# Twelve state groups of a selective scan: states into PSUM, C products from GpSimd to VectorE

## The chip, the core and the metric

The kernel runs on one core of a Trainium2 chip. The metric is the device time of the whole program in microseconds (us), the median of several runs. Engines are named as in the profile: PE is TensorE, PEld its weight loads, DVE is VectorE, ACT is ScalarE, POOL is GpSimd, SP is SyncE, which here starts nearly all DMAs.

## What is computed

Two layers of an image network on a tensor of 4 batches, 384 channels and 32 x 32 positions, all in float32. The first layer is a selective scan in four directions followed by a mixture of experts (4 experts, 2 per token); the second is self-attention (8 heads of 64) followed by a feed-forward part. The change lies in the scan. Cut to that part, the reference is:

```python
xs = cross_scan(x)                       # 4 directions, 384 channels, 1024 positions
x_dbl = einsum('bkdl,kcd->bkcl', xs, x_proj_weight)
dts, Bs, Cs = split(x_dbl, [12, 16, 16])
dt = softplus(einsum('bkrl,kdr->bkdl', dts, dt_projs_weight) + bias)
for l in range(1024):                    # 16 states n of each channel d
    h = h * exp(dt[l] * A) + (dt[l] * u[l]) * B[l]
    y[l] = sum_n(h * C[l])
```

Here A is one number per channel and state. After it come the sum of the directions, a normalisation, GELU and the residual.

## The kernel before

**Layout of the scan.** The 384 channels are 12 blocks of 32 channels; the 16 states are 4 *state groups* (NG) of 4 states. A block of 32 channels with 4 states fills the 128 partitions. A *unit* is a batch, a direction k (in the order 0, 1, 3, 2) and a half i of the 1024 positions (512 each), so a batch has 8 units; directions 2 and 3 run through the halves and the positions backwards. A unit has 3 *chunks* c of 128 channels (4 blocks, two pairs q), and each chunk goes through the 4 state groups g. A batch thus has 96 state groups (8 units x 3 chunks x 4), each with 4 blocks.

**One state group** (`chunk`, from L436): for each pair q, GpSimd multiplies dt times u with B for both blocks in one instruction (bx, L445, 128x1024). For each block j, ScalarE makes the decay exp(dt A) into a PSUM bank (da, L454); there are two such banks. VectorE runs the recurrence over 512 positions as a scan (L459), from zero or from the carried state of the half before. In the first half of a direction VectorE copies the last state to a small carry tile (L470 for q = 0, L465 for q = 1). Then the states are multiplied by C. For q = 0 the scan writes the states over bx in SBUF, and GpSimd multiplies both blocks by C in one instruction (L473, 128x1024). For q = 1 the scan writes the states over the decay in PSUM, and VectorE multiplies each block by C (L466, 128x512). GpSimd does not read PSUM anywhere in this kernel. At last four TensorE matmuls with a 0/1 matrix (L480) sum over the states into the chunk's accumulator acc (a PSUM bank), over the 4 groups. There are 6 buffers for bx, 7 for the loaded dt and dt times u (dtr), and 2 shared PSUM banks ("ps") for acc and the projections.

**Around it** (`scan_layer`): after a chunk's last group VectorE adds acc to y (L291 for direction 0, L295 for the others). The next unit's projection (`project`) is interleaved with the groups: a matmul for dt (L370), ScalarE steps of a softplus (L374 to L387), in the first batch TensorE sums (L383), in later batches GpSimd subtractions (L400, L401) and a VectorE addition (L407), then dt times x on VectorE (L408), and DMAs to and from DRAM (L410, L411, L429). After the last direction of a half, `finish` normalises and stores it (GpSimd addition L239).

**Order of the work.** A scheduler places each instruction in its engine's queue by a modelled timeline and priorities; each engine then runs its queue in that order. The rest of the network for batch b (the *tail*: routing, experts from L991 and L1013, attention from L1123, feed-forward) is placed after the scan of batch b and is interleaved with the scan of batch b + 1. In the first batch no tail runs beside the scan; the tail of the last batch runs alone at the end.

Of the kernel before, what the change touches and what calls it, by code (L numbers as in the profile page):

```python
# [58 lines left out]
NG = NS // NJ  # L59
# [58 lines left out]
class Body:  # L118
# [295 lines left out]
    def chunk(self, unit, first, c, fed, carry, nega, sel, acc, work, dap):  # L414

        nc = self.nc
        b, k, i = unit
        bcs, dd, _ = fed  # L420
        dtr = []
        for q in range(NJ // 2):

            pair = []
            at = c * P + q * 2 * DB
            for s in range(2):
                t = work.tile([P, 2, HF], F32, tag="dtr", name="dtr", bufs=7)
                for n in range(NJ):
                    nc.sync.dma_start(  # L429
                        out=t[n * DB : (n + 1) * DB],  # L430
                        in_=dd[s, at : at + 2 * DB, :].rearrange("(j d) l -> d j l", d=DB),
                    )
                pair.append(t)
            dtr.append(pair)

        def run(ap):  # L436
            return ap[:, ::-1] if k >= 2 else ap

        last = 0 if k >= 2 else HF - 1
        for g in range(NG):  # L440
            bc = bcs[g]
            out = []
            for q in range(NJ // 2):
                bx = work.tile([P, 2, HF], F32, tag="bx", name="bx", bufs=6)
                pool = nc.gpsimd.tensor_mul(  # L445
                    bx, dtr[q][1], bc[:, 0].unsqueeze(1).to_broadcast([P, 2, HF])
                ).ins
                cg = bc[:, 1]
                at = ((c * 2 + q) * NG + g) * 2
                for j in range(2):  # L450
                    block = c * NJ + 2 * q + j
                    col = (k * NB + block) * NG + g
                    da = dap.tile([P, HF], F32, tag="da", name="da")
                    nc.scalar.activation(  # L454
                        da, dtr[q][0][:, j, :], AF.Exp, scale=nega[:, col : col + 1]
                    )
                    hold = carry[:, at + j : at + j + 1]
                    h = bx[:, j, :] if q == 0 else da
                    nc.vector.tensor_tensor_scan(  # L459
                        run(h), run(da), run(bx[:, j, :]), 0.0 if first else hold,  # L460
                        ALU.mult, ALU.add,
                    )
                    if q == 1:
                        if first:
                            nc.vector.tensor_copy(hold, h[:, last : last + 1])  # L465
                        dve = nc.vector.tensor_mul(bx[:, j, :], h, cg).ins  # L466
                if q == 0:
                    if first:
                        for j in range(2):
                            nc.vector.tensor_copy(  # L470
                                carry[:, at + j : at + j + 1], bx[:, j, last : last + 1]
                            )
                    pool = nc.gpsimd.tensor_mul(  # L473
                        bx, bx, cg.unsqueeze(1).to_broadcast([P, 2, HF])
                    ).ins
                out.append(bx)
            for q in range(NJ // 2):
                for j in range(2):
                    lo = (2 * q + j) * DB
                    nc.tensor.matmul(  # L480
                        acc[lo : lo + DB, :], sel, out[q][:, j, :],
                        start=(g == 0), stop=(g == NG - 1),
                    )
            self.place_behind = {"pool": pool, "dve": dve}
            yield
# [1089 lines left out]
```

## Time and profile before

| what | value |
|---|---|
| median of 3 runs | 4209.68 us (4201.19 to 4214.02) |
| the profiled execution's own time | 4199.62 us |
| its span in the trace | 4197.9 us |
| mean granted TensorE clock | 0.877 |
| first GpSimd product of the scan starts | 44.13 us |
| seventh unit's last sum into y (VectorE) | 641.07 us |

The page of the profile has these slices (40 equal ones of 105 us; each digit is the busy share in tenths, 9 for 90% or more):

```profile
PE   6545454479987888789996887789996988999899
DVE  5999997878887877788887867788887862010101
ACT  5555555556665776776665776676665774421353
POOL 5999997898989877798989976888998961000100
PEclk8666666589998999799998998789998999999999
```

Three stages can be seen. Slices 2 to 7 or so are the first batch's scan, in which GpSimd and VectorE are busy and TensorE is half idle at a low granted clock. Then scan and tail run together, up to about slice 33. The last seven slices are the tail of the last batch, in which GpSimd and VectorE do nearly nothing. A busy row gives the engine's time, its share of the span and the number of instructions; a group's row gives line, engine, operation, output and inputs with shapes, the count, then busy time and mean ns of one, then the idle time of the engine just before these instructions and what ended most of it. TensorE has two records for each matmul.

### The profile page before, as it was taken

What the parts mean: (1) busy time and instruction counts of PE and PEld (TensorE: products, weight loads), DVE (VectorE), ACT (ScalarE), POOL (GpSimd) and SP (SyncE); (2) the same over time, 40 slices, a digit from 0 to 9 for tenths busy, and PEclk for the clock granted to TensorE, in tenths of its full rate; (3) what the DMA queues carried; (4) which work ended last, traced back from release to release, by engine and by line L of the source; (5) the groups of instructions that cost most, each with busy time, mean ns of one, the idle gap of its engine ahead of it and who ended that gap; (6) DMA issues with size and microseconds to landing.
All of it is one profiled execution on the core that took longest, in us unless ns stands there. A gap on an engine that the chain in (4) does not pass through costs nothing. (4 is left out here: it accounts for less than half of the span.)

```text
span 4197.9 us, 45862 instructions
## 1 busy us (share of the span) xinstructions
PE 3348.0 (80%) x13372; PEld 1574.9 (38%) x13372; DVE 2872.9 (68%) x4250; ACT 2463.8 (59%) x4485; POOL 3022.8 (72%) x1476
## 2 busy tenths in 40 slices
PE   6545454479987888789996887789996988999899
PEld 2101111145553223255553223245563224577423
DVE  5999997878887877788887867788887862010101
ACT  5555555556665776776665776676665774421353
POOL 5999997898989877798989976888998961000100
PEclk8666666589998999799998998789998999999999
DMA  5554464577986444577886434568887424356200
GB/s 139 126 136 124 111 176 111 154 226 217 254 249 179 103 131 120 170 213 228 233 252 192 112 105 137 153 195 241 224 249 220 109 64 170 122 179 208 88 6 31
DMA packets 378883, 677.67 MB, mean 161 GB/s; under 512 B 49920, under 2 KB 179328, under 8 KB 378624
## 3 DMA queue, kind: packets, MB, share of 16 engines
q1 hardware_dynamic: 368800, 647.42, 54.1%
q0 software_dynamic: 8192, 25.21, 1.9%
q8 instruction: 108, 1.77, 0.2%
q10 hardware_dynamic: 1632, 2.04, 0.2%
q14 instruction: 151, 1.24, 0.1%
HBM read 566.68 MB, written 107.79 MB: 161 GB/s over the span
## 5 line engine op out<-in xcount | busy, mean ns | idle before, releaser
L445 POOL TENSOR_TENSOR bx<-dtr,bcs 128x1024 f32<-128x1024 f32 x768 | 1795.4, 2365 | 189.1 <-PE acc L480 103.1
L454 ACT ACTIVATE da<-dtr,nega 128x512 f32<-128x512 f32 x1536 | 1044.5, 690 | 921.1 <-DVE bx L466 568.3
L473 POOL TENSOR_TENSOR bx<-bx,bcs 128x1024 f32<-128x1024 f32 x384 | 907.2, 2366 | 138.3 <-DVE carry L470 69.2
L480 PE MATMUL acc<-bx,sel 128*32 128x512 f32 x3072 | 495.4, 707 | 320.8 <-POOL bx L473 294.6
L991 PE MATMUL h_ps<-xc,w 128*128 128x256 f32 (+1 forms) x3168 | 652.3, 361 | 45.6 <-DMA w<-in_w 18.4
L1013 PE MATMUL y_ps<-w,hs 128*128 128x384 f32 x1824 | 630.2, 497 | 26.9 <-ACT hs L1004 18.7
L991 PEld LDWEIGHTS h_ps<-xc,w 128*128 128x128 f32 x3168 | 547.4, 196 | 202.4 <-issue 87.0
L459 DVE TENSOR_TENSOR_SCAN bx<-da,carry,bx 128x512 f32<-128x512 f32 x384 | 474.1, 1270 | 118.2 <-POOL bx L445 64.8
L459 DVE TENSOR_TENSOR_SCAN da<-da,carry,bx 128x512 f32<-128x512 f32 x384 | 475.9, 1273 | 77.6 <-ACT da L454 68.7
L459 DVE TENSOR_TENSOR_SCAN bx<-da,bx 128x512 f32<-128x512 f32 x384 | 451.9, 1210 | 95.1 <-POOL bx L445 54.7
L466 DVE TENSOR_TENSOR bx<-da,bcs 128x512 f32<-128x512 f32 x768 | 509.4, 680 | 3.9 <-DMA bcs<-both 0.4
L459 DVE TENSOR_TENSOR_SCAN da<-da,bx 128x512 f32<-128x512 f32 x384 | 455.2, 1218 | 68.8 <-ACT da L454 55.5
L1013 PEld LDWEIGHTS y_ps<-w,hs 128*128 128x128 f32 x1824 | 345.1, 193 | 305.3 <-issue 56.1
L1146 PE MATMUL s_ps<-w 64*128 64x512 f32 x1024 | 311.2, 663 | 76.6 <-ACT ex L1152 72.2
L1152 ACT ACTIVATE ex<-s_ps 128x512 f32<-128x512 f32 x512 | 300.7, 591 | 107.3 <-PE s_ps L1146 105.7
L1044 POOL DMA_INDIRECT got<-made,g_source x64 | 61.2, 957 | 401.1 <-PE h_ps L991 381.4
L999 ACT ACTIVATE hs<-h_ps,bb 128x256 f32<-128x256 f32 (+1 forms) x528 | 200.4, 441 | 240.5 <-PE h_ps L991 178.5
L1195 PE MATMUL o_acc<-ex,vt 128*64 128x512 f32 x1024 | 287.5, 639 | 23.2 <-ACT ex L1152 20.8
L480 PEld LDWEIGHTS acc<-bx,sel 128*32 128x32 f32 x3072 | 73.9, 116 | 611.2 <-POOL bx L473 404.8
L1146 PEld LDWEIGHTS s_ps<-w 64*128 64x128 f32 x1024 | 83.6, 190 | 287.3 <-ACT ex L1152 235.7
L370 PE MATMUL dt_ps<-xd,wdt 108*128 108x512 f32 x192 | 124.7, 736 | 59.5 <-ACT mag L409 30.5
L1017 DVE TENSOR_TENSOR y<-y_ps,bb 128x384 f32<-128x384 f32 x76 | 41.7, 549 | 170.0 <-PE y_ps L1013 170.0
(240 smaller groups left out, 3594.2 us busy)
## 6 DMA issues: line engine op xcount, KB each, us to landing
w<-in_w SPq DMA_DIRECT2D x352, 576.0 KB
dtr<-dd SPq DMA_DIRECT2D x1536, 128.0 KB
bcs<-both SPq DMA_DIRECT2D x512, 128.0 KB
dd<-one_e SPq DMA_DIRECT2D x96, 256.0 KB
dd<-mag SPq DMA_DIRECT2D x96, 256.0 KB
xt<-x SPq DMA_DIRECT2D x32, 384.0 KB
made<-y SPq DMA_DIRECT2D x32, 384.0 KB
xs<-rows SPq DMA_DIRECT2D x28, 385.0 KB
```

The lines of the kernel that those rows point to most:

```text
L445: pool = nc.gpsimd.tensor_mul(bx, dtr[q][1], bc[:, 0].unsqueeze(1).to_broadcast([P, 2, HF])).ins
L454: nc.scalar.activation(da, dtr[q][0][:, j, :], AF.Exp, scale=nega[:, col : col + 1])
L459: nc.vector.tensor_tensor_scan(run(h), run(da), run(bx[:, j, :]), 0.0 if first else hold, ALU.mult, ALU.add,)
L466: dve = nc.vector.tensor_mul(bx[:, j, :], h, cg).ins
L473: pool = nc.gpsimd.tensor_mul(bx, bx, cg.unsqueeze(1).to_broadcast([P, 2, HF])).ins
L480: nc.tensor.matmul(acc[lo : lo + DB, :], sel, out[q][:, j, :], start=(g == 0), stop=(g == NG - 1),)
L991: ins = nc.tensor.matmul(ps[:, r, :], w1[(f + r) // wf][:, c, (f + r) % wf * P : ((f + r) % wf + 1) * P], xc[:, c, :], start=(c == 0), sto ...
L999: done = nc.scalar.activation(hs[:, f + r, :], ps[:, r, :], AF.Gelu if last or alone else AF.Identity, bias=bb[:, f + r : f + r + 1],).ins
L1013: nc.tensor.matmul(out[:, :D], hs[:, f, t * P : (t + 1) * P], w2[f // wf][:, f % wf, :], start=(f == 0), stop=(f == FC - 1),)
L1146: ins = nc.tensor.matmul(ps, w[rows, j * P : (j + 1) * P], w[rows, halves(i)], start=True, stop=True).ins
L1152: done.append(nc.scalar.activation(ex[:, o, :], ps, AF.Exp, scale=HD**-0.5, accum_out=sums[:, t, 2 * j + o, i : i + 1],).ins)
L1195: ins = nc.tensor.matmul(out[cols, :], made[t][1][:, j, cols], ex[:, o, :], start=(j == 0), stop=(j == MB - 1),).ins
```

## The change

In the first batch (b = 0), in the last state group of a chunk (g = NG - 1), and where c + i < 2 (chunks 0 and 1 of half 0, chunk 0 of half 1, which is 3 of the 6 chunks of each direction, 12 in all), the pair q = 0 is treated as q = 1 is: the scan writes its states over the decay in PSUM, the carry is copied from there, and VectorE multiplies each block by C. The GpSimd product by C of that pair is gone. The rest of the program is the same; the scheduler orders it anew.

```diff
         for g in range(NG):
             bc = bcs[g]
             out = []
+            spare = b == 0 and g == NG - 1 and c + i < 2
             for q in range(NJ // 2):
+                in_psum = q == 1 or spare
...
                     hold = carry[:, at + j : at + j + 1]
-                    h = bx[:, j, :] if q == 0 else da
+                    h = da if in_psum else bx[:, j, :]
                     nc.vector.tensor_tensor_scan(
...
-                    if q == 1:
+                    if in_psum:
                         if first:
                             nc.vector.tensor_copy(hold, h[:, last : last + 1])
                         dve = nc.vector.tensor_mul(bx[:, j, :], h, cg).ins
-                if q == 0:
+                if not in_psum:
                     if first:
                         for j in range(2):
                             nc.vector.tensor_copy(
```

## The prediction

> **What bounds the kernel now.** I read the busy rows and the slices of the page first, then a table of 210 us stretches, then what VectorE and GpSimd wait for inside the first batch, then a few microseconds of VectorE in order of time. The page and its groups:
>
> ```profile
> PE 3348.0 (80%) x13372; PEld 1574.9 (38%) x13372; DVE 2872.9 (68%) x4250; ACT 2463.8 (59%) x4485; POOL 3022.8 (72%) x1476
> L445 POOL TENSOR_TENSOR bx<-dtr,bcs 128x1024 f32<-128x1024 f32 x768 | 1795.4, 2365 | 189.1 <-PE acc L480 103.1
> L473 POOL TENSOR_TENSOR bx<-bx,bcs 128x1024 f32<-128x1024 f32 x384 | 907.2, 2366 | 138.3 <-DVE carry L470 69.2
> L459 DVE TENSOR_TENSOR_SCAN bx<-da,carry,bx 128x512 f32<-128x512 f32 x384 | 474.1, 1270 | 118.2 <-POOL bx L445 64.8
> L459 DVE TENSOR_TENSOR_SCAN da<-da,carry,bx 128x512 f32<-128x512 f32 x384 | 475.9, 1273 | 77.6 <-ACT da L454 68.7
> L466 DVE TENSOR_TENSOR bx<-da,bcs 128x512 f32<-128x512 f32 x768 | 509.4, 680 | 3.9 <-DMA bcs<-both 0.4
> ```
>
> The whole-span shares mislead: TensorE leads only because it works alone after 3500 us. The stretches (busy time of each engine in each) show it:
>
> ```profile
> 210.00:420.00 210.00, 98.31 (x316) 22.99 (x312) 193.06 (x261) 110.86 (x173) 208.95 (x91) 0.64 0.50 130
> 420.00:630.00 210.00, 104.97 (x322) 26.63 (x322) 194.63 (x273) 111.55 (x174) 208.96 (x92) 0.66 0.54 144
> 1050.00:1260.00 210.00, 192.88 (x891) 121.83 (x891) 173.55 (x240) 139.17 (x223) 188.01 (x88) 0.97 0.88 252
> 3570.00:3780.00 210.00, 210.00 (x815) 137.20 (x814) 20.20 (x34) 68.63 (x111) 0.00 (x0) 1.00 0.48 152
> ```
>
> The columns are TensorE, weight loads, VectorE, ScalarE, GpSimd, then the granted TensorE clock, DMA share and GB/s. In the first batch, where nothing of the tail runs beside the scan, GpSimd is busy 208.95 of 210 us (99.5%) and VectorE 193 to 195 (92%). The first batch's scan runs from GpSimd's first product at 44 us to about 778 us. From 850 to 3400 us scan and tail overlap and no engine is full; after that TensorE is alone. The change works in the first batch, so that is the stage to read. How near is VectorE to being the bound there? What it waited for between 121 and 641 us (total us, times, longest):
>
> ```profile
> DVE bx L459 <- ACT da L454: 10.2, 51, 0.3
> DVE da L459 <- ACT da L454: 9.3, 8, 2.4
> DVE y L295 <- PE acc L480: 8.9, 9, 1.7
> DVE one_e L408 <- PE dt_ps L383: 4.5, 6, 1.2
> DVE y L291 <- PE acc L480: 3.3, 3, 1.8
> DVE bx L459 <- POOL bx L445: 2.8, 5, 1.8
> ```
>
> Busy there is 478.3 of 520 us. The 51 waits of 0.2 us belong to VectorE's own loop: there are two PSUM banks for the decays, so the next decay can be computed only when the product has let a bank go. In order of time, one state group:
>
> ```profile
> 308.95 1.27 DVE L466 TENSOR_TENSOR bx<-da,bcs 128x512 f32<-128x512 f32 x2
> 310.45 2.46 DVE L459 TENSOR_TENSOR_SCAN bx<-da,carry,bx 128x512 f32<-128x512 f32 x2 [0.24 <-ACT da L454]
> 312.83 2.44 DVE L459 TENSOR_TENSOR_SCAN da<-da,carry,bx 128x512 f32<-128x512 f32 x2
> 315.18 1.27 DVE L466 TENSOR_TENSOR bx<-da,bcs 128x512 f32<-128x512 f32 x2
> ```
>
> From product pair to product pair is 6.23 us: two scans into SBUF, two into PSUM, two products, and one gap of 0.24 us. GpSimd needs three products of 2.31 us each for a group (by starts: six took 13.93 us), 6.93 us. So the two engines stand 6.2 to 6.9, and VectorE also carries about 2 us per chunk of four groups (y, dt times x).
>
> **The change, part by part.** All 12 groups are the last group of a chunk; they lie in three of every six chunks of the first batch.
>
> *Taken from GpSimd:* 12 C products (L473) of 2.31 us, 27.7 us. All lie on the busy engine, but two of the twelve are in the scan's first unit (44 to about 140 us, by 48 scans), where GpSimd itself waited 7.5 us for VectorE.
>
> *Added to VectorE:* 24 products of 128x512. Two take 1.27 us in the lines above, and records overlap by some 0.08 us, as with the scans (2.44 us long, 2.35 from start to start), so 1.19 us a pair, 14.3 us. With them comes a second gap per group: the next block's decays wait for these products as they do for the others, 0.2 us by the 51 waits above, 2.4 us in all. Sum 16.7 us, or 1.4 us a group. The four blocks of a group then hold PSUM banks through scan and product; nothing else uses those two banks, so TensorE is not held by it.
>
> *Moved:* the scans' target, SBUF to PSUM. The rows say 1270 ns into bx and 1273 ns into da: 0.003 x 24 = 0.1 us. The Trainium skill speaks against the change here: Perfetto Trace Analysis, Optimizing Scalar/DVE Operations, gives a VectorE operation about 60 ns of access overhead on SBUF and about 125 ns on PSUM. By that rule 24 scans would cost 1.6 us more. The row is for the same instruction with only the target changed, so I take 0.1 us. The same section warns that offloading between VectorE and GpSimd might not help, as they share an SBUF read port. If each added product held GpSimd up for its length, 14.3 us of the 27.7 would be lost. SBUF — State Buffer, Who interferes with whom, narrows that to VectorE instructions with two SBUF inputs; the product reads h in PSUM and only C in SBUF. GpSimd's products took 2332 to 2427 ns in the first 660 us, beside 173 such VectorE products, which leaves no room for stalls of 0.6 us. I take nothing.
>
> *Waits:* the carry copies stay as many, from PSUM at 149 ns, from SBUF at 153 (medians of the first 660 us): nothing. The matmuls of the last group no longer wait for a GpSimd product. VectorE's y waits for the chunk's accumulation, which ends with just that product (12.2 us in 12 waits above): these waits should go in the changed chunks, and shrink in the others, since GpSimd comes ahead. The 4.5 us on dt_ps are of the same kind: that matmul stands in TensorE's queue behind accumulations that wait for GpSimd. DMAs stay as many. In the order of instructions, GpSimd makes six bx products in a row at the start of many chunks and then three C products; all six bx buffers are then out, so what is late next is VectorE's scans.
>
> **The sum, by stretch.** From 121 to 641 us (the first unit's last chunk and the units 2 to 7, with 8 changed groups) GpSimd would need 517.9 - 8 x 2.31 = 499 us. VectorE needs 478.3 busy, plus its own gaps (75 groups, as L473 runs 75 times there, x 0.2 = 15), plus 8 x 1.4 = 11: 504.5 us. So VectorE becomes the bound, and at best 520 - 504.5 = 15.5 us are gained. The queues are in fixed order, only three groups are buffered, and changed chunks (VectorE 4 x 6.23 + 2 + 1.4 = 28, GpSimd 11 x 2.31 = 25.4 us) lie among others (27 against 27.7), so I leave some 5.5 us of waits, about half of the 12.2 on y: gain 10 us. First unit: VectorE is already what GpSimd waits for; two changed groups here cost up to 2.8 us, partly covered by VectorE's own 5.7 us of waits for bx: loss 1 us. Last unit (682 to 778 us): GpSimd is full, as it also makes the next batch's softplus subtractions; two C products less, 4.6 us, VectorE has 13 of 118 us idle: gain 3 us. Between them, from 641 to 682 us, normalisation and loading of the next batch keep both waiting; that is a chain of its own and only moves earlier. Together 12 us, off the profiled execution's 4199.6 us (span 4197.9): 4187.6. The median of the runs shown is 4209.7, 10 us above that execution; the same gain gives 4198 us.
>
> What lies after is moved earlier whole if the order stays. It does not quite: TensorE's stream has the accumulations up to 75 places later among the tail's matmuls while the third batch is scanned, and the fourth batch's first normalisation 30 places later. I take nothing for that, and put it into the range.
>
> **The rivals.**
> 1. *The whole relief counts* (chance 0.22). If most of VectorE's gaps are only GpSimd's shadow, GpSimd stays the bound: 10 groups (8, and 2 in the last unit) x 2.31 = 23, less 1 in the first unit, 22 us, 4188 us. For it: 99.5% busy, no waits. Against: the gaps of 0.2 us wait for ScalarE, not GpSimd.
> 2. *VectorE was the bound in all but name* (0.15). Then gain and added work cancel: within 4 us, 4206 to 4212 us. For it: 92% plus 3% of own gaps. Against: 12.2 us of y waits.
> 3. *The new order costs more later* (0.19). One mechanism: in the third batch TensorE's queue holds accumulations behind up to 75 more of the tail's matmuls. The trace has two records to a matmul (3072 for 1536 accumulations), and the experts' first matmuls (L991) take 652.3 us for 3168 / 2, 0.41 us each; that is up to 31 us once, during which all six bx buffers stay taken, so GpSimd stops and then VectorE. Between 900 and 3400 us GpSimd already waits 85.7 us in 23 waits for such matmuls, the longest 16.9. A slowdown begins when more than 12 us is added; with 31, 4229 us. Against: tail matmuls that come earlier leave the queue emptier later.
> 4. *The change does not do what it says*: excluded by the order of instructions, which has 12 products less on GpSimd and 24 more on VectorE.
>
> **How the numbers follow.** The likeliest case, VectorE becoming the bound, has 0.44, with a gain of 6 to 17 us (4193 to 4204). A measurement of this kernel can tell about 0.3%, 12.6 us, from no change. Of the likeliest case 0.22 lies beyond that, with rival 1 it makes 0.44 faster; its other 0.22, rival 2 and the mild end of rival 3 (0.01) make 0.38 the same; the rest of rival 3 is 0.18 slower. Range: 4178 (rival 1 and a favourable order) to 4224 (most of rival 3).
>
> **What would show it.** In the changed profile L473 should have 372 instructions and L466 792, at unchanged 2366 and 680 ns. From 210 to 630 us VectorE should rise to 96 to 98% and GpSimd fall to about 96%; y waits should shrink below 6 us between 121 and 641 us; the seventh unit's last y, 641.07 us now, should come about 9 us earlier. Wrong would be: GpSimd still at 99% (rival 1), that time unmoved (rival 2), or an early gain that is lost after 900 us in GpSimd's waits for accumulations (rival 3).

## The result, and the profile after

| | before | after |
|---|---|---|
| median | 4205.4 us (5 runs) | 4314.73 us (5 runs) |
| ratio, 95% interval | | 1.0264 [1.025, 1.0279] |
| the profiled execution's own time (span) | 4199.62 us (4197.9) | 4320.2 us (4318.4) |

The changed kernel is 2.6% slower, about 110 us, where 12 us faster had been forecast. The median before differs from the 4209.7 us above because two more runs came in. The busy row and four groups of the page after (lines above 444 are shifted by 2 in the code):

```profile
PE 3383.0 (78%) x13372; PEld 1594.9 (37%) x13372; DVE 2909.5 (67%) x4274; ACT 2461.4 (57%) x4483; POOL 2994.1 (69%) x1464
L447 POOL TENSOR_TENSOR bx<-dtr,bcs 128x1024 f32<-128x1024 f32 x768 | 1791.3, 2361 | 229.2 <-PE acc L482 144.8
L475 POOL TENSOR_TENSOR bx<-bx,bcs 128x1024 f32<-128x1024 f32 x372 | 875.7, 2360 | 230.8 <-DVE carry L472 133.9
L461 DVE TENSOR_TENSOR_SCAN da<-da,carry,bx 128x512 f32<-128x512 f32 x396 | 491.7, 1274 | 90.6 <-ACT da L456 67.5
L468 DVE TENSOR_TENSOR bx<-da,bcs 128x512 f32<-128x512 f32 x792 | 525.7, 680 | 3.8
```

The work is as predicted: 12 C products less on GpSimd, 24 more on VectorE, and none of these instructions takes over 1 ns longer (2360, 1274, 680 ns; 2366, 1273, 680 before). What grew is the idle time in front of GpSimd's instructions, behind the second bar: 189.1 to 229.2 us before bx, 138.3 to 230.8 before the C products. In stretches of 210 us (columns as in the prediction):

```profile
210.00:420.00 210.00, 102.56 (x300) 24.33 (x292) 187.08 (x244) 101.60 (x159) 188.05 (x82) 0.68 0.46 120
420.00:630.00 210.00, 108.97 (x303) 26.49 (x304) 191.43 (x264) 109.77 (x171) 191.41 (x83) 0.72 0.50 129
```

In the first batch both engines are less busy than before: GpSimd 188 to 191 us for 209, and VectorE, which has more to do, 187 to 191 for 193 to 195. Neither is full, so neither is the bound. What VectorE and GpSimd waited for between 121 and 641 us (total us, times, longest) shows that they wait for each other; "carry" is the small copy right behind VectorE's scans, so a wait for it is a wait for the scans:

```profile
DVE bx L461 <- POOL bx L447: 13.4, 13, 2.2
DVE y L295 <- PE acc L482: 6.9, 8, 1.9
DVE da L461 <- POOL bx L447: 6.2, 4, 2.2
```

```profile
POOL bx L475 <- DVE carry L472: 22.3, 9, 3.9
POOL bx L475 <- DVE bx L461: 18.6, 8, 3.8
POOL bx L447 <- DMA dtr<-dd: 9.3, 4, 4.4
```

GpSimd waits 40.9 us for VectorE, in 17 waits, and VectorE 19.6 us for GpSimd's bx, also in 17. The third row, 9.3 us for the load of dt, is not the cause: it stands in run 5 below too (9.4 us), which loses nothing. Before, VectorE had waited 3.5 us for GpSimd's bx in this stretch, and GpSimd once for VectorE:

```profile
POOL bx L473 <- DVE carry L470: 1.1, 1, 1.1
```

One such place in the timeline after, GpSimd first:

```profile
256.14 4.66 POOL L447 TENSOR_TENSOR bx<-dtr,bcs 128x1024 f32<-128x1024 f32 x2
262.24 9.28 POOL L447 TENSOR_TENSOR bx<-dtr,bcs 128x1024 f32<-128x1024 f32 x4 [1.44 <-PE acc L482]
271.48 2.36 POOL L475 TENSOR_TENSOR bx<-bx,bcs 128x1024 f32<-128x1024 f32 x1
274.29 2.36 POOL L475 TENSOR_TENSOR bx<-bx,bcs 128x1024 f32<-128x1024 f32 x1 [0.46 <-DVE carry L472]
280.58 2.34 POOL L475 TENSOR_TENSOR bx<-bx,bcs 128x1024 f32<-128x1024 f32 x1 [3.93 <-DVE carry L472]
282.88 18.52 POOL L447 TENSOR_TENSOR bx<-dtr,bcs 128x1024 f32<-128x1024 f32 x8
```

```profile
282.42 0.68 DVE L468 TENSOR_TENSOR bx<-da,bcs 128x512 f32<-128x512 f32 x1
285.27 2.35 DVE L461 TENSOR_TENSOR_SCAN da<-da,bx 128x512 f32<-128x512 f32 x2 [2.17 <-POOL bx L447]
```

GpSimd has made the bx products of three groups in a row (all six buffers) and then makes their three C products. The third has to wait for VectorE's scans of its group (3.93 us). Only after it does GpSimd go on to the next group's bx, so VectorE, done with its products, waits 2.17 us in its turn. In the order of instructions GpSimd's queue had 3 runs of five or more bx in the first batch before, and has 23 after.

When VectorE starts the last sum into y of a unit tells where the loss arises. The two profiled executions differ by 120.5 us in span; 112.3 of them are there when the scan of the last batch ends (us):

| last sum of | before | after | later by |
|---|---|---|---|
| first batch, unit 2 | 222.8 | 235.1 | 12.3 |
| first batch, unit 7 | 641.1 | 677.5 | 36.4 |
| first batch, unit 8 | 759.3 | 810.6 | 51.3 |
| second batch, unit 8 | 1657.8 | 1734.8 | 77.0 |
| third batch, unit 8 | 2565.0 | 2660.4 | 95.3 |
| fourth batch, unit 8 | 3432.0 | 3544.3 | 112.3 |

More than half arises in the batches that the change doesn't touch. There, from 900 to 3510 us, GpSimd waits more than the kernel before did from 900 to 3400 us (85.7, 54.2 and 47.3 us for the same three; run 10 shows these rows):

```profile
POOL bx L447 <- PE acc L482: 119.8, 31, 20.1
POOL bx L475 <- DVE carry L472: 92.2, 38, 7.6
POOL bx L475 <- DVE bx L461: 64.4, 32, 5.4
```

### The profile page after: what moved, and what is told of

Same layout as the page of the kernel before. It is cut to its first block, busy times and chain, and to the rows that moved or that the text cites. A ratio compares the mean times of both kernels' runs of the same rounds, so it can differ in the third digit from the quotient of the medians.

```text
span 4318.4 us, 45877 instructions
## 1 busy us (share of the span) xinstructions
PE 3383.0 (78%) x13372; PEld 1594.9 (37%) x13372; DVE 2909.5 (67%) x4274; ACT 2461.4 (57%) x4483; POOL 2994.1 (69%) x1464
## 5 line engine op out<-in xcount | busy, mean ns | idle before, releaser
L447 POOL TENSOR_TENSOR bx<-dtr,bcs 128x1024 f32<-128x1024 f32 x768 | 1791.3, 2361 | 229.2 <-PE acc L482 144.8
L475 POOL TENSOR_TENSOR bx<-bx,bcs 128x1024 f32<-128x1024 f32 x372 | 875.7, 2360 | 230.8 <-DVE carry L472 133.9
L482 PE MATMUL acc<-bx,sel 128*32 128x512 f32 x3072 | 517.4, 706 | 307.6 <-POOL bx L475 243.0
L1015 PE MATMUL y_ps<-w,hs 128*128 128x384 f32 x1824 | 642.4, 505 | 48.4 <-ACT hs L1006 38.7
L461 DVE TENSOR_TENSOR_SCAN bx<-da,carry,bx 128x512 f32<-128x512 f32 x372 | 458.8, 1270 | 150.2 <-POOL bx L447 85.3
L461 DVE TENSOR_TENSOR_SCAN da<-da,carry,bx 128x512 f32<-128x512 f32 x396 | 491.7, 1274 | 90.6 <-ACT da L456 67.5
L468 DVE TENSOR_TENSOR bx<-da,bcs 128x512 f32<-128x512 f32 x792 | 525.7, 680 | 3.8
L461 DVE TENSOR_TENSOR_SCAN bx<-da,bx 128x512 f32<-128x512 f32 x372 | 439.7, 1210 | 114.6 <-POOL bx L447 72.2
L461 DVE TENSOR_TENSOR_SCAN da<-da,bx 128x512 f32<-128x512 f32 x396 | 471.8, 1219 | 57.3 <-ACT da L456 41.2
L1197 PE MATMUL o_acc<-ex,vt 128*64 128x512 f32 x1024 | 288.1, 638 | 28.1 <-ACT ex L1154 18.5
```

Of the source, the lines that this page charges most:

```text
L447: pool = nc.gpsimd.tensor_mul(bx, dtr[q][1], bc[:, 0].unsqueeze(1).to_broadcast([P, 2, HF])).ins
L461: nc.vector.tensor_tensor_scan(run(h), run(da), run(bx[:, j, :]), 0.0 if first else hold, ALU.mult, ALU.add,)
L475: pool = nc.gpsimd.tensor_mul(bx, bx, cg.unsqueeze(1).to_broadcast([P, 2, HF])).ins
L482: nc.tensor.matmul(acc[lo : lo + DB, :], sel, out[q][:, j, :], start=(g == 0), stop=(g == NG - 1),)
L1015: nc.tensor.matmul(out[:, :D], hs[:, f, t * P : (t + 1) * P], w2[f // wf][:, f % wf, :], start=(f == 0), stop=(f == FC - 1),)
L1197: ins = nc.tensor.matmul(out[cols, :], made[t][1][:, j, cols], ex[:, o, :], start=(j == 0), stop=(j == MB - 1),).ins
```

## The experiments

Two theories stood against each other: **O**, the scheduler's new order of the queues costs, the moved work nothing; **V**, VectorE's load costs. A third, **D**: a late first batch drags the others behind it. The change alters both the instructions and, through the scheduler, the order of all queues. To part them, the order was taken from the schedule of one kernel and imposed on the instructions of the other. The edit, the same in all kernels whose order is called pinned:

```diff
+def pinned(tc, nc, order):
+    traced = list(nc.cur_bb.bb.instructions)
+    how = mybir.DependencyInfo(mybir.DependencyClass.NoSync, mybir.DependencyReason.DATA)
+    for engine, text in order.items():
+        mine = [i for i in traced if str(i.engine).split(".")[-1] == engine]
+        at, before = 0, None
+        for step in array.array("h", zlib.decompress(base64.b85decode(text))):
+            at += step
+            if before is not None:
+                tc.add_manual_dep(mine[at], before.name, how, reason="order")
+            before = mine[at]
...
+        pinned(tc, nc, ORDER_OF)
         over = nc.values_load(flag[0:1, 0:1], min_val=0, max_val=1)
```

These edges fix only the order within a queue; no wait for another engine is added or taken. ORDER_OF holds one list of places per engine. The kernel before, pinned to its own order and otherwise unchanged, has no run of its own, but run 10 is just that up to 850 us: its first batch ends 1.6 us later (760.9 against 759.3), so the pinning itself costs next to nothing.

**1. The new instructions in the old order.**

> The changed kernel's instructions, every engine's queue pinned to the order of the kernel before; the 24 new products stand right behind their scans, the 12 GpSimd products are missing. If the new order is what costs (theory O), the loss goes and the predicted gain shows: 4190 to 4205 us, the seventh unit's last y at 630 to 636 us. If VectorE's added load itself costs (theory V), about 4300 us, that y near 677 us as in the changed kernel.

Measured: 4209.83 us against 4205.86 for the kernel before, ratio 1.0006 [0.9995, 1.0016]. The loss is gone, so V falls as the cause of the 110 us. The predicted gain is not there either. The stretch from 121 to 641 us, in the kernel before and here:

```profile
121.00:641.00 520.00, 254.97 (x796) 62.29 (x796) 478.34 (x636) 274.92 (x428) 517.91 (x225) 0.65 0.52 135
```

```profile
121.00:641.00 520.00, 256.35 (x784) 64.35 (x788) 484.50 (x648) 272.49 (x424) 494.15 (x215) 0.66 0.50 132
```

GpSimd fell from 517.9 to 494.2 us of 520 and VectorE rose to 484.5, yet the seventh unit's last y came 5.9 us later (647.0, where 630 to 636 had been expected).

**2. The old instructions in the new order.**

> The instructions of the kernel before, every queue pinned to the order of the changed kernel; each of the 12 C products stands on GpSimd behind the next group's first bx. Theory O: 4315 to 4350 us (the loss of the changed kernel, and 12 products more on GpSimd). Theory V: about 4205 us.

Measured: 4324.13 us, ratio 1.0279 [1.0263, 1.0295]. The instructions of the kernel before, without any of the change, are as slow as the changed kernel when they stand in its order.

**3 and 4. The order by parts.** The same, with the order changed over at the last scan of the first batch.

> The changed kernel in its own order until the last scan of the first batch, then pinned to the order of the kernel before. If each stretch's order costs for itself (theory O), only the first batch's loss of 36 to 45 us stays: 4240 to 4255 us. If a late first batch drags the later ones behind it (theory D), 4300 us or more.

Measured: 4256.29 us, ratio 1.0113 [1.0097, 1.0129].

> The changed kernel pinned to the order of the kernel before until the last scan of the first batch, then in its own order. Theory O: the 65 to 75 us that the later batches lost stay, less the gain of the first batch: 4255 to 4280 us. Theory D: about 4200 us.

Measured: 4274.77 us, ratio 1.0165 [1.0149, 1.0181]. The new instructions with the old order stood at 1.0006; the new order adds 1.07% in the first batch and 1.59% after it. With the 0.06% of the instructions that makes 2.72%, and the changed kernel has 2.64%: within the intervals the parts add up. A first batch that ends 48 us late hardly drags the others: in run 3 the delay was 47.9 us at its end and 55.6 at the end of the last. D falls. A lower TensorE clock does not explain the first batch's part: run 3's mean granted clock was 0.880 to 0.883, no lower than the 0.875 to 0.881 of the kernel before beside it. Run 4's was a little lower, 0.874 to 0.879 (0.873 to 0.874 in the changed kernel, where TensorE is busy 35 us longer for as many records); whether that is a cause or a result of the waits, no run tells.

**5. One rule in the first batch.** The scheduler is free again, with an edge for GpSimd's bx alone (last_c, set in a line not shown, is the group's C product, or nothing where the group has none):

```diff
+                with self.behind_c(b == 0):
-                pool = nc.gpsimd.tensor_mul(
-                    bx, dtr[q][1], bc[:, 0].unsqueeze(1).to_broadcast([P, 2, HF])
-                ).ins
+                    pool = nc.gpsimd.tensor_mul(
+                        bx, dtr[q][1], bc[:, 0].unsqueeze(1).to_broadcast([P, 2, HF])
+                    ).ins
...
+            self.c_products = [*self.c_products[-1:], last_c]
...
+    def behind_c(self, on):
+        if not on or len(self.c_products) < 2 or self.c_products[0] is None:
+            return nullcontext()
+        return self.tc.issue_after(self.c_products[0])
```

> The changed kernel with one rule for the first batch: the bx products of a state group are queued on GpSimd behind the C product of the group two before it; the scheduler does the rest. Every later batch then stands in exactly the order of the kernel before. If GpSimd's runs of six bx and three C products are the cause in the first batch (theory R), its 36 us go: 4195 to 4215 us, no difference from before that can be told. If VectorE's load in the first batch costs (theory V), 4235 us or more.

Measured: 4196.5 us against 4192.84, ratio 1.0007 [0.9995, 1.0019]. All 110 us are gone with a rule on one queue of one batch. It does this in two ways. In the first batch GpSimd's queue has 5 runs of five or more bx instead of 23. And in the later batches, which the rule doesn't touch, the scheduler now comes to the order of the kernel before: from 742 us on TensorE, VectorE, ScalarE and GpSimd have their instructions in the same order in both traces. The stretch from 121 to 641 us:

```profile
121.00:641.00 520.00, 263.58 (x798) 67.55 (x796) 493.18 (x659) 275.47 (x430) 500.01 (x217) 0.68 0.53 137
```

Here VectorE is at 493.2 us (95%), GpSimd at 500. Up to the seventh unit 4.7 us are gained (y at 636.4), the transition to the second batch comes earlier by as much, and in the eighth unit the gain is lost (761.2 against 759.3).

**6. The bunching alone.** The kernel before, pinned to its own order, with GpSimd's queue in the units 2 to 7 rewritten from b C b b b C b b C b b C per chunk (b for bx) to b b b b b b C C C.

> The instructions and the order of the kernel before, with one change: in the units 2 to 7 of the first batch GpSimd's queue is regrouped to six bx and then three C products, 24 times. Theory R: the first batch loses 30 to 45 us, 4235 to 4255 us. If GpSimd's order is harmless and other queues' order costs, below 4215 us.

Measured: 4260.18 us, ratio 1.0161 [1.0135, 1.0187], 59.8 us lost by the seventh unit. That is above the 30 to 45 us expected. Bunching is enough to cost what the first batch lost; that it costs more here than the 36 us in the changed kernel may come from the other queues, which were ordered along with GpSimd's there and stand as before here. GpSimd's C products now wait for VectorE's scans, and VectorE's y, which stands at its old place, waits for acc, to which the late C products lead (143 to 690 us):

```profile
POOL bx L473 <- DVE carry L470: 23.1, 5, 6.9
POOL bx L473 <- DVE bx L459: 22.5, 5, 6.9
DVE y L295 <- PE acc L480: 45.8, 9, 7.2
DVE bx L459 <- POOL bx L445: 13.5, 13, 2.1
```

**7. One group of twelve.** `spare = b == 0 and g == NG - 1 and c + i == 0 and k == 0`, the scheduler free.

> Only one of the twelve groups is changed (direction 0, chunk 0, half 0), the scheduler is free. By the work alone 1.4 us more on VectorE: 4207 us. Theory O (what the scheduler makes of a shifted timeline decides): the first two units, where GpSimd's queue is bunched, lose 5 to 10 us, the later batches change by tens of us either way, so anything from 4210 to 4310 us and not 4207.

Measured: 4255.52 us, ratio 1.0147 [1.0124, 1.017], some 62 us. In the profiled execution, the slowest of the four (4270.2 us), the first batch lost 6 us (unit 2: 6.7, unit 7: 6.2), since the bunching dies out after two units; the batches after it lost 62 more by the last y. One changed group, by the prediction's sum about 1.4 us of work, gave the later batches another order, and that cost 1.3%. Part of the cost may lie on ScalarE: in this order its queue has 142 loads of a function table (ACT_TABLE_LOAD in the profile), 15 more than before, at 1.28 us each. The changed kernel has 125 loads, two less than before, so its own loss has another source.

**8. The rule in all batches**, in the kernel before and in the changed one.

> The kernel before with the rule in all batches: bx of a group behind the C product of the group two before it, the scheduler does the rest. If runs of bx also cost in the later batches: faster, 4150 to 4195 us. If there the room to run ahead covers waits for TensorE: slower, 4215 to 4260 us.

Measured: 4205.47 us against 4192.84, ratio 1.0035 [1.002, 1.0049]. Neither of the two ranges: the later batches neither gain from the rule nor lose much.

> The changed kernel with the rule for bx in all batches. The later batches of the kernel before under this rule lost 8 us net; if the rule fixes the order there too, the new instructions change nothing: 1.003 to 1.005 of the kernel before. If the order of the later batches is again another one, any value from 0.995 to 1.02.

Measured: 4223.56 us against 4203.77, ratio 1.0043 [1.0028, 1.0058]. Next to 1.0035 the new instructions again change nothing that can be told.

**9. Relief and load apart**, both pinned to the old order, to see why the gain of run 1 is missing:

```diff
-                    pool = nc.gpsimd.tensor_mul(
-                        bx, bx, cg.unsqueeze(1).to_broadcast([P, 2, HF])
-                    ).ins
+                    if not (b == 0 and g == NG - 1 and c + i < 2):
+                        pool = nc.gpsimd.tensor_mul(
+                            bx, bx, cg.unsqueeze(1).to_broadcast([P, 2, HF])
+                        ).ins
```

> The kernel before in its own order, with the twelve C products left out on GpSimd and put nowhere (the states of these blocks go unmultiplied into the sum). The relief alone. If GpSimd was the bound of the first batch: 18 to 23 us gained there, about 0.995 of the kernel before. If VectorE was as near to being the bound as its waits for ScalarE say (15 us of its 41 us idle): 8 us gained or less, 0.998 to 1.000.

Measured: 4195.87 us against 4203.77, ratio 0.9984 [0.9975, 0.9993], 6.7 us by the ratio.

```diff
                         dve = nc.vector.tensor_mul(bx[:, j, :], h, cg).ins
+                        if b == 0 and g == NG - 1 and c + i < 2:
+                            dve = nc.vector.tensor_mul(bx[:, j, :], h, cg).ins
```

> The kernel before in its own order, with 24 VectorE products more: in the same twelve groups each product of the pair q = 1 is made twice (the same value into the same place), and GpSimd keeps all its work. The load alone. If VectorE had room: within 4 us, 1.000 to 1.001. If it had none: 14 to 17 us in the first batch, 1.003 to 1.004.

Measured: 4215.37 us, ratio 1.0025 [1.0015, 1.0035], 10.5 us, between the two ranges. Over the whole time relief and load together make 1.0009, and run 1 found 1.0006. In the first batch alone they don't add: at the y of its eighth unit the relief gave 8.6 us and the load took 4.6, which would be a gain of 4, and run 1, with both, was 4.0 us late. What run 1 has besides is the second wait for a decay in each changed group; from 121 to 641 us VectorE waits 22.3 us for decays (70 waits) where it had waited 19.5 us (59 waits). That is 3 of the 8 us; the rest stays open. So does the rest of the load's time, which arose later (10.5 us late at the end of the second batch, 18.5 at the end of the third).

**10. TensorE's order in the later batches.** The kernel before in its own order; on TensorE alone, from the second batch's first expert matmul on, the accumulations of a chunk's first three groups stand up to two tail matmuls later (by the trace some 740 accumulations moved, most of them by two).

> The kernel before in its own order, but from the second batch's first tail matmuls on, on TensorE alone, the accumulations of a chunk's first three groups stand up to two of the tail's matmuls later. By the third rival of the prediction (accumulations behind tail matmuls keep the bx buffers taken) GpSimd's waits for acc grow from 86 us, and the run is 10 to 40 us slower. If GpSimd is not sensitive to them: within 5 us.

Measured: 4267.07 us against 4203.77, ratio 1.0139 [1.0124, 1.0153], far above the 10 to 40 us. GpSimd's waits from 900 to 3400 us, before and here:

```profile
POOL bx L445 <- PE acc L480: 85.7, 23, 16.9
POOL bx L473 <- DVE carry L470: 54.2, 21, 8.6
POOL bx L473 <- DVE bx L459: 47.3, 22, 6.7
```

```profile
POOL bx L445 <- PE acc L480: 146.0, 35, 15.9
POOL bx L473 <- DVE carry L470: 52.2, 20, 8.6
POOL bx L473 <- DVE bx L459: 33.7, 17, 4.2
```

The row for acc alone grows by 60 us, about what the run lost (58). The mechanism of the third rival is real and steep. In the changed kernel that row grew by 34 us and the two rows for VectorE by 55, so its later loss is not that mechanism alone. Which queue's order makes how much of it stays open.

## Why the prediction was wrong

**Bound now.** Half right. GpSimd was at 99.5% and almost without waits, but taking 27.7 us from it is worth 6.7 us (run 9). VectorE, at 92% and with gaps of its own, was nearly as close to the bound; the prediction's sum had seen this (504.5 of 520 us) and still left 10 us of gain.

**The added and the removed work.** The counts and durations were right, the 0.003 us for the scans' target too (1274 ns into PSUM, 1270 into SBUF). The 1.6 us that the prediction estimated from the Trainium skill (Perfetto Trace Analysis, Optimizing Scalar/DVE Operations) are not seen; the scan reads its decay from PSUM in both forms, so its output alone may not call for them. GpSimd's products did not get longer, so the warning of the shared port did not apply. The terms of the sum were mis-sized: together they are worth +2.5 us (1.0006, interval from -2 to +7 us), not -12. The step that failed there was "I leave some 5.5 us of waits, about half of the 12.2 on y: gain 10 us". In the old order the seventh unit's y came 5.9 us later (run 1); in a fitting order 4.7 us were gained by the seventh unit (run 5). "Last unit: gain 3 us" failed as well: in run 5 the last unit lost the 4.7 us again and 1.9 us more; GpSimd waited 6.5 us for VectorE there (677 to 800 us), where the kernel before had waited 1.2 us (682 to 800 us). For the instructions alone, rival 2 was right.

**The order.** The step that decided was "What lies after is moved earlier whole if the order stays. It does not quite: ... I take nothing for that". After the first batch the new order is worth 1.59% (about 67 us). In the first batch it is worth 1.07% (about 45 us), and there the prediction had even read it: "GpSimd makes six bx products in a row at the start of many chunks and then three C products; all six bx buffers are then out, so what is late next is VectorE's scans". It gave this no price. The price stood in the trace before: two of its three such runs lie in the first unit, and each ends in a wait of GpSimd for VectorE's scans, of 3.08 and 1.12 us:

```profile
68.47 2.35 POOL L473 TENSOR_TENSOR bx<-bx,bcs 128x1024 f32<-128x1024 f32 x1 [3.08 <-DVE carry L470]
118.98 2.36 POOL L473 TENSOR_TENSOR bx<-bx,bcs 128x1024 f32<-128x1024 f32 x1 [1.12 <-DVE carry L470]
```

Twenty more at 2.1 us would have been an estimate of 42 us. After the change GpSimd's waits for VectorE between 121 and 641 us are 40.9 us, and the seventh unit comes 36.4 us late.

**The rivals.** Rival 3 named the side on which it ended and a real mechanism, but as one stall of at most 31 us with a chance of 0.19. Run 10 shows that it isn't one stall: some 740 accumulations, most of them two places later, cost 58 us. GpSimd is busy 90% of the time in those batches too (188.0 of 210 us from 1050 to 1260 us), and its waits for acc are waits for the bx buffers that late accumulations hold. The bunching in the first batch, the other half, was in no rival.

**What would show it.** The signs set down answered clearly: GpSimd at 90 to 91% in place of 96, the seventh unit's y later by 36.4 us instead of earlier by 9, and growing waits for acc after 900 us. The first two together (less busy and later) speak against all of rivals 1 to 3 for the first batch and point to the order; the proof is in runs 1 to 6.

## What to carry to other kernels

Where a scheduler places the instructions, a small edit has two effects: its own work, and a new order of every queue behind it. Read the second as carefully as the first: look for changed runs of one instruction in a queue (here b b b b b b C C C), ask which buffers such a run exhausts and who waits for the last of it, and price it in each repetition. To judge an edit's own worth, pin the order or constrain the queue that bunches; here that took the 110 us off and showed that the edit itself is worth nothing that can be told (1.0006 and 1.0007). An engine at 99.5% beside one at 92% with gaps of its own left little to be gained: even the relief without the load gave 0.16%.

## What was not expected of the hardware

How little slack this buffered pipeline of four engines has: moving TensorE's accumulations behind about two other matmuls (about 0.4 us each, by 652.3 us for 1584 of the experts' first matmuls) cost 58 us. And how much of a time can hang on a detail elsewhere: one group of the first batch's 96, about 1.4 us of VectorE work at 80 us of the run, moved the end by 62 us, nearly all of it after the first batch. The work itself is too small for that; what it changed is the order of the queues.
